# A graph layer with a guessed order of edges: the verdict on dst over the 180 real groups, and mids cleared first

## The chip, the core and the metric

The kernel runs on one core of a Trainium2 chip, in one launch. The metric is the device time of an execution in microseconds (us). Before the change the median of three executions is 5790.02 us (5788.27 to 5802.1). In the text PE is TensorE, PEld its weight load, DVE VectorE, ACT ScalarE, POOL GpSimd and SP SyncE; a small q behind an engine's name means its sequencer, which issues transfers.

## The reference

One graph layer with 12500 nodes of 128 numbers and 412500 edges of 48 numbers; dst is sorted.

```python
h   = relu(layernorm(x))                                    # 12500 x 128
agg = segment_sum(edge_attr_48, dst, num_segments=12500)    # 12500 x 48
u   = graph_globals[0]                                      # all nodes are in graph 0
z   = concatenate([h, agg, u])
out = x + relu(z @ W1 + b1) @ W2 + b2
```

## The kernel before

The kernel holds two programs for the same result. The **guessed program** (lines 129 to 497) runs first and always. It relies on dst being sorted and nearly evenly spread: edges are taken in chunks of 768 (128 partitions by 6), three chunks make a group, and there are 179 full groups and one tail of 84 edges, `NG = 180` in all. A group's edges are expected to fall into a window of 32 nodes for each chunk. For each group DVE compares the places of the edges inside the window with an iota (`onehot`, line 207), PE multiplies edges with that table (`aggregate`, line 219, 36 instructions in the trace, 18 in the program), and DVE adds the window into `aggT`, the sums by node, at an offset that it reads from the row `at_i` (`add`, line 229). Blocks of 512 nodes go through layernorm and the two matrix products in between (lines 231 to 336), and are stored to `out`.

The **general program** (lines 503 to 609) stands under `tc.If(isbad >= 1)`. It clears `aggT` and recomputes everything without a guess: a loop over 537 chunks (line 569) with an inner loop over windows of 64 nodes (line 556), and then a loop over 125 blocks of 100 nodes (line 577). It writes `out` again.

What decides between them is `bad`, a number that `verdict` (line 379) makes from the table `chk`: the largest entry of each of the 128 rows, summed over the rows by PE and clamped to 0..1. Fourteen of the 15 columns of `chk` hold sums of how far edges fall outside their windows (`outside`, line 186, on ACT). The last column is written by `places` (line 356). It takes the row `mids`, dst in the middle of each group, subtracts the expected middle `cen`, clamps the difference to plus or minus `SLACK = 47`, and puts the largest square of what was cut off into `chk` (line 365). The same lines make `at_i`. These rows have `NGP = 187` places, since `cen` is an iota in rows of 11; there are 180 groups, so seven places are padding.

The order on each engine is that of the code (`tc.manual_schedule`); semaphores hold an instruction until the ones that it depends on are done, and each transfer has one of eight semaphore lanes and waits for the transfer before it on its lane. What matters at the start:

- SP's queue loads the middles `md` and the rows `di` of dst, the edges `e` of the first groups and the block `xt` of x.
- ACT's queue loads `mids` in two pieces (lines 392 and 395). ACT then copies the transposed places of the first 30 chunks to `rel` (line 182), issues eight loads of weights (lines 339 to 347, among them `u`, line 346), and makes the first check (line 188).
- POOL makes the constants, clears `mids` (line 409), `chk` and `w1a`, and then clears `aggT` in 16 pieces (line 426), 14 of them ahead of its first other work.
- DVE makes `df`, the places relative to the window (line 173), the table of group 0 (line 207), then `places` with the cast of `mids` at line 358, then the table of group 1.
- PE transposes `df` (line 181), takes group 0 and group 1, then the product of `u` with its weights (line 353), then group 2.

Of the kernel before, what the change touches and what calls it, by code (L numbers as in the profile page):

```python
# [11 lines left out]
OP = mybir.AluOpType  # L12
AX = mybir.AxisListType
# [8 lines left out]
def kernel(  # L22
# [12 lines left out]
    nc = tc.nc  # L35
# [22 lines left out]
    NG = NGF + 1  # L58
# [71 lines left out]
    with fast:  # L130
# [12 lines left out]
        NCK = 2 * len(parts) + 2  # L143
        chk = one.tile([P, NCK + 1], F32)
        offrow = one.tile([1, 126], F32)
        off = one.tile([126, 1], F32)
        mids = one.tile([1, NGP], I32)
        cen = one.tile([1, NGP], F32)
        dev = one.tile([1, NGP], F32)
        devc = one.tile([1, NGP], F32)  # L150
# [4 lines left out]
        def load_dst(i):  # L155
            c0, rows = parts[i]
            di = dp.tile([126, CE], I32, name="di")
            md = dp.tile([126, 1], I32, name="md")
            with nc.allow_non_contiguous_dma(reason="one number a row"):
                nc.sync.dma_start(  # L160
                    md[:rows],
                    dst[c0 * CE:(c0 + rows) * CE].rearrange("(g e) -> g e", e=GE)[:, GE // 2:GE // 2 + 1]
                    .to_broadcast([rows // CG, CG]))
            nc.sync.dma_start(di[:rows], dst[c0 * CE:(c0 + rows) * CE].rearrange("(c e) -> c e", e=CE))
            dsts[i] = di, md
# [190 lines left out]
        def places():  # L356
            mf = one.tile([1, NGP], F32)
            nc.vector.tensor_copy(mf, mids)
            nc.vector.tensor_tensor(dev, mf, cen, OP.subtract)
            nc.vector.tensor_scalar(devc, dev, float(-SLACK), float(SLACK), OP.max, OP.min)  # L360
            nc.vector.tensor_tensor(mf, devc, cen, OP.add)
            nc.vector.tensor_scalar(at_i, mf, 0.0, float(N - 1), OP.max, OP.min)
            nc.vector.tensor_tensor(dev, dev, devc, OP.subtract)
            nc.vector.tensor_tensor(devc, dev, dev, OP.mult)
            nc.vector.tensor_reduce(chk[0:1, NCK:NCK + 1], devc, AX.X, OP.max)

        def tail_dst():
            di = one.tile([P, T], I32)
# [19 lines left out]
        AHEAD = 9  # L388
        with tc.manual_schedule():
            load_dst(0)  # L390
            with nc.allow_non_contiguous_dma(reason="a number a group, once"):
                nc.scalar.dma_start(
                    mids[:, :NGF],
                    dst[:NGF * GE].rearrange("(a g e) -> a g e", a=1, e=GE)[:, :, GE // 2])
                nc.scalar.dma_start(
                    mids[:, NGF:NG], dst[None, NCH * CE + TAIL // 2:NCH * CE + TAIL // 2 + 1])
# [9 lines left out]
            nc.gpsimd.memset(over, float(1 - W))  # L406
            nc.gpsimd.iota(cen, pattern=[[SPAN, NGP // PER], [EACH, PER]], base=HALF, channel_multiplier=0,
                           allow_small_or_imprecise_dtypes=True)
            nc.gpsimd.memset(mids, 0)
            nc.gpsimd.memset(chk, 0.0)  # L410
            nc.gpsimd.memset(w1a, 0.0)
            warm = one.tile([P, 1], F32)
# [23 lines left out]
            for g in range(3, AHEAD):  # L436
                load(g)
            onehot(0)
            places()
            onehot(1)  # L440
            load_weights()
# [196 lines left out]
```

## Time and profile before

| | |
|---|---|
| median of three executions | 5790.02 us |
| the profiled execution | 5793.29 us |
| its span, first to last instruction | 5791.3 us |
| instructions | 139158 |
| busy: PE, PEld, DVE, ACT, POOL | 1728.0, 1342.1, 1069.6, 352.7, 58.6 us |
| moved from and to memory | 175.00 and 12.80 MB |
| granted TensorE clock, mean | 0.532 |

The profile is of one execution. The busy times are shares of a span that has stages with different limits, so they are read stage by stage: from the span's start, the guessed program, then the general program's preparation, its loop over chunks and its loop over blocks, each a window of time. Lines of the kernel name the stage: numbers under 500 are the guessed program, numbers from 512 on the general one.

### The profile page before, as it was taken

How to read it: one execution, taken by the hardware profiler on the slowest of the kernel's cores; microseconds unless marked ns; L12 is line 12 of the kernel's file. 1: busy time of each engine (PE TensorE's matmuls, PEld its weight loads, DVE VectorE, ACT ScalarE, POOL GpSimd, SP SyncE). 2: the span in 40 equal slices, each digit the busy share in tenths (PEclk: the TensorE clock that was granted, in tenths of full speed). 3: DMA queues.
4: the chain of work that ended last, by engine and by line, in shares of the span. 5: the costliest groups of instructions: out<-in, count | busy, mean ns of one | idle time of the engine just before them, and what ended most of it. 6: DMA issues, size and time to landing. Idle time of an engine off the chain costs nothing. (4 is left out here: it accounts for less than half of the span.)

```text
span 5791.3 us, 139158 instructions
## 1 busy us (share of the span) xinstructions
PE 1728.0 (30%) x15319; PEld 1342.1 (23%) x15320; DVE 1069.6 (18%) x3730; ACT 352.7 (6%) x902; POOL 58.6 (1%) x58
## 2 busy tenths in 40 slices
PE   8962222222222222222222222222223333333333
PEld 6741111111111111111111111111122222222222
DVE  6641111111111111111111111111111111111111
ACT  3320000000000000000000000000001111111111
POOL 2010000000000000000000000000000000000000
PEclk9975555555555555555555555555555555555555
DMA  9830000000000000000000000000000000000000
GB/s 287 277 109 20 20 21 20 20 20 20 20 21 20 20 20 20 20 21 21 20 20 20 20 21 21 20 20 20 20 14 8 8 8 8 8 8 8 8 8 8
DMA packets 186921, 188.97 MB, mean 33 GB/s; under 512 B 16241, under 2 KB 179625, under 8 KB 186843
## 3 DMA queue, kind: packets, MB, share of 16 engines
q1 hardware_dynamic: 185541, 187.36, 10.9%
q8 instruction: 58, 0.95, 0.1%
q10 hardware_dynamic: 1302, 0.49, 0.0%
q14 instruction: 20, 0.16, 0.0%
HBM read 175.00 MB, written 12.80 MB: 32 GB/s over the span
## 5 line engine op out<-in xcount | busy, mean ns | idle before, releaser
L564 PE MATMUL ps<-oh,e 128*48 128x64 f32 x6456 | 815.0, 316 | 3043.1 <-DVE oh L560 3043.1
L564 PEld LDWEIGHTS ps<-oh,e 128*48 128x48 f32 x6456 | 699.9, 198 | 3157.9 <-DVE oh L560 3157.9
L555 DVE TENSOR_SCALAR r<-rel 128x6 f32 x537 | 92.5, 172 | 1323.6 <-PEq L569 1322.8
L592 PE MATMUL pt<-ident,xn 100*128 100x100 f32 x125 | 53.5, 428 | 857.1 <-ACT xn L590 857.1
L560 DVE TENSOR_TENSOR oh<-iota,r 128x384 f32<-128x384 f32 x538 | 300.5, 559 | 18.4
L567 DVE TENSOR_TENSOR aggT<-aggT,ps 48x64 f32 x538 | 115.3, 214 | 902.2 <-PE ps L564 902.2
L558 DVE TENSOR_SCALAR r<-r 128x6 f32<-128x6 f32 x538 | 92.6, 172 | 1013.7 <-DMA e<-in_edge_attr_dram 1010.5
L548 ACT COPY relt<-pt 14x1 f32<-14x1 f32 x6 | 0.9, 148 | 3857.7 <-POOLq L551 3856.4
L592 PEld LDWEIGHTS pt<-ident,xn 100*128 100x128 f32 x125 | 22.7, 182 | 899.4 <-ACT xn L590 899.4
L600 PE MATMUL ph<-hT,w1h 128*128 128x100 f32 x500 | 187.2, 478 | 95.8 <-ACT hid L602 54.3
L601 PE MATMUL ph<-ag,w1a 48*128 48x100 f32 x500 | 186.6, 475 | 0.0
L219 PE MATMUL ps<-oh,e 128*48 128x32 f32 x6456 | 176.0, 212 | 16.6 <-DVE oh L207 11.1
L219 PEld LDWEIGHTS ps<-oh,e 128*48 128x48 f32 x6456 | 161.3, 128 | 63.7 <-issue 24.2
L607 DVE TENSOR_TENSOR ot<-po,xt 100x128 f32<-100x128 f32 x125 | 36.5, 292 | 731.0 <-PE po L605 731.0
L600 PEld LDWEIGHTS ph<-hT,w1h 128*128 128x128 f32 x500 | 125.2, 310 | 157.6 <-ACT hid L602 85.2
L605 PE MATMUL po<-w,hid 128*100 128x128 f32 x500 | 156.7, 469 | 0.0
L207 DVE TENSOR_TENSOR oh<-iota,rel 128x576 f32<-128x576 f32 x179 | 151.0, 844 | 2.4 <-ACT rel L182 2.2
L601 PEld LDWEIGHTS ph<-ag,w1a 48*128 48x128 f32 x500 | 124.8, 310 | 44.4 <-issue 44.4
L605 PEld LDWEIGHTS po<-w,hid 128*100 128x100 f32 x500 | 101.8, 264 | 34.5 <-issue 22.2
L602 ACT ACTIVATE hid<-ph,bias 128x100 f32<-128x100 f32 x250 | 86.0, 344 | 378.9 <-PE ph L601 378.9
L596 DVE COPY ag<-aggT 128x100 f32 x125 | 26.6, 213 | 335.1 <-PEq L577 333.6
L586 ACT ACTIVATE sc<-mv,eps 100x1 f32<-100x1 f32 x125 | 36.8, 295 | 801.9 <-DVE mv L585 801.9
(103 smaller groups left out, 892.0 us busy)
## 6 DMA issues: line engine op xcount, KB each, us to landing
e<-in_edge_attr_dram SPq DMA_DIRECT2D x179, 432.0 KB
e<-in_edge_attr_dram SPq DMA_DIRECT2D x537, 144.0 KB
xt<-in_x_dram SPq DMA_DIRECT2D x125, 50.0 KB
out_dram<-ot SPq DMA_DIRECT2D x125, 50.0 KB
xt<-in_x_dram SPq DMA_DIRECT2D x24, 256.0 KB
out_dram<-ot SPq DMA_DIRECT2D x24, 256.0 KB
di<-in_dst_dram SPq DMA_DIRECT2D x4, 384.0 KB
di<-in_dst_dram SPq DMA_DIRECT2D x4, 378.0 KB
```

The lines of the kernel that those rows point to most:

```text
L207: nc.vector.tensor_tensor(oh[:k, :n], iota[:k, None, :W].to_broadcast([k, n, W]), r[:, :, None].to_broadcast([k, n, W]), OP.is_equal)
L219: nc.tensor.matmul(ps[h:h + DE, at:at + W], e[:k, c, t * DE:(t + 1) * DE], oh[:k, c * T + t, :], start=(c == 0 and t < 2), stop=(c == n - ...
L555: nc.vector.tensor_scalar(r[:k], r_view, float(WA), None, OP.add)
L558: nc.vector.tensor_scalar(r[:k], r[:k], float(-WA), None, OP.add)
L560: nc.vector.tensor_tensor(oh[:k], iota[:k, None, :].to_broadcast([k, T, WA]), r[:k, :, None].to_broadcast([k, T, WA]), OP.is_equal)
L564: nc.tensor.matmul(ps, e[:k, t * DE:(t + 1) * DE], oh[:k, t, :], start=(t == 0), stop=(t == T - 1))
L567: nc.vector.tensor_tensor(to, to, ps, OP.add)
L592: nc.tensor.transpose(pt[:, :BA], xn[:BA], ident[:BA, :BA])
L600: nc.tensor.matmul(ph, w1h[:, h * P:(h + 1) * P], hT, start=True, stop=False)
L601: nc.tensor.matmul(ph, w1a[:DE, h * P:(h + 1) * P], ag[:DE], start=False, stop=True)
L602: nc.scalar.activation(hid[:, h], ph, AF.Relu, bias=bias[:, h:h + 1])
L605: nc.tensor.matmul(po[:BA], hid[:, h], w2[:, h], start=(h == 0), stop=(h == NH - 1))
```

## The change

`places` takes the largest square over `devc[:, :NG]`, the 180 real places, and no longer over all 187. The clearing of `mids` stands right behind `load_dst(0)`, ahead of the two loads into `mids` and of all of POOL's other work.

```diff
@@ places()
             nc.vector.tensor_tensor(devc, dev, dev, OP.mult)
-            nc.vector.tensor_reduce(chk[0:1, NCK:NCK + 1], devc, AX.X, OP.max)
+            nc.vector.tensor_reduce(chk[0:1, NCK:NCK + 1], devc[:, :NG], AX.X, OP.max)
@@ the start of the schedule
             load_dst(0)
+            nc.gpsimd.memset(mids, 0)
             with nc.allow_non_contiguous_dma(reason="a number a group, once"):
                 nc.scalar.dma_start(
                     mids[:, :NGF],
...
                            allow_small_or_imprecise_dtypes=True)
-            nc.gpsimd.memset(mids, 0)
             nc.gpsimd.memset(chk, 0.0)
```

On POOL, at the start of the program, before the change (offrow, ones, ident, iota and cen are constants; DMAHW names a transfer's semaphore lane):

```order
L397 ISA
L397 IOTA offrow 1x126
L399 MEMSET ones 128x1
L400 MEMSET ident 128x128
L401 AFFINE_SELECT ident<-ident 128x128 [waits Pool_49]
L403 IOTA iota 128x64
L405 MEMSET eps 128x1
L406 MEMSET over 128x1
L407 IOTA cen 1x187
L409 MEMSET mids 1x187 [waits DMAHW2_49,DMAHW0_49]
L410 MEMSET chk 128x15
L411 MEMSET w1a 128x256
```

And the same place with the change:

```order
L391 MEMSET mids 1x187
L398 ISA
L398 IOTA offrow 1x126
L400 MEMSET ones 128x1
L401 MEMSET ident 128x128
L402 AFFINE_SELECT ident<-ident 128x128 [waits Pool_49]
L404 IOTA iota 128x64
L406 MEMSET eps 128x1
L407 MEMSET over 128x1
L408 IOTA cen 1x187
L410 MEMSET chk 128x15
L411 MEMSET w1a 128x256
```

The clearing of `mids` moved to the front, and with it went POOL's wait for the two loads of `mids`; from `cen` on POOL now waits for nothing. In both programs the first 14 pieces of `aggT` (line 426) are the next rows.

On ACT, the start of its program with the change (w1h to b_sb are weights and biases; pt is the transposed df):

```order
L393 DMA mids<-in_dst_dram 1x179x1 [waits Pool_49]
L396 DMA mids<-in_dst_dram 1x1
L413 ACT_TABLE_LOAD
L413 ACTIVATE warm<-eps 128x1 [waits Pool_49]
L182 COPY rel<-pt 128x3x30 [waits PE_49] x2
L339 DMA w1h<-in_L_gnn_W_dram 128x256 [waits DMAHW4_49]
L340 DMA w1a<-in_L_gnn_W_dram 48x256 [waits DMAHW5_49,Pool_49]
L341 DMA w1a<-in_L_gnn_W_dram 48x256 [waits DMAHW7_49]
L342 DMA w1u<-in_L_gnn_W_dram 64x256 [waits DMAHW0_49]
L343 DMA w_71<-in_L_gnn_W_dram 128x2x128 [waits DMAHW1_49]
L345 DMA b_sb<-in_L_gnn_b_dram 128x2x1 [waits DMAHW3_49]
L346 DMA u<-in_L_gnn_graph_globals_dram 64x1 [waits DMAHW4_49]
```

Its order is as before; what is new is that the first load of `mids` waits for POOL, and that lanes have changed hands (line 341 waited for lane 6 before).

On DVE, around the cast of `mids` (mf is its copy in f32), before with a minus and after with a plus:

```order
-L171 TENSOR_TENSOR sub<-md,off 30x1 [waits DMAHW1_49,DVE_49]
-L173 TENSOR_SCALAR df<-di,sub 30x768 [waits DMAHW3_49,DVE_49]
+L171 TENSOR_TENSOR sub<-md,off 30x1 [waits DMAHW0_49,DVE_49]
+L173 TENSOR_SCALAR df<-di,sub 30x768 [waits DMAHW2_49,DVE_49]
 L207 TENSOR_TENSOR oh<-iota,rel 128x576 [waits Activation_49,Pool_49]
-L358 CAST mf<-mids 1x187 [waits DMAHW2_49,DMAHW0_49,Pool_49]
-L359 TENSOR_TENSOR dev<-mf,cen 1x187 [waits DVE_49]
+L358 CAST mf<-mids 1x187 [waits DMAHW3_49,DMAHW1_49]
+L359 TENSOR_TENSOR dev<-mf,cen 1x187 [waits DVE_49,Pool_49]
```

Nothing moved on DVE: the cast waits for the loads of `mids` alone, where it waited for POOL's clearing too.

## Rows read from the trace of the kernel before

**Rows 1.** The page's first line: span and instructions.

```profile
span 5791.3 us, 139158 instructions
```

**Rows 2.** Windows by stage: us, busy us (instructions) of each engine, PEclk, DMA share, GB/s.

```profile
32.00:365.00 333.00, 321.56 (x6901) 245.40 (x6898) 223.09 (x617) 117.35 (x222) 33.88 (x24) 1.00 0.80 260
...
414.00:4277.00 3863.00, 816.05 (x6462) 700.44 (x6462) 600.94 (x2152) 0.89 (x6) 0.00 (x0) 0.50 0.07 20
4277.00:5788.00 1511.00, 557.76 (x1625) 374.58 (x1625) 199.55 (x875) 214.70 (x625) 0.00 (x0) 0.50 0.03 8
```

**Rows 3.** Page, costliest groups: busy us, mean ns, idle before, who ended it.

```profile
L564 PE MATMUL ps<-oh,e 128*48 128x64 f32 x6456 | 815.0, 316 | 3043.1 <-DVE oh L560 3043.1
...
L555 DVE TENSOR_SCALAR r<-rel 128x6 f32 x537 | 92.5, 172 | 1323.6 <-PEq L569 1322.8
```

**Rows 4.** The instructions of line 503: ns min/median/max, first and last start.

```profile
L503 SPq COMPARE_BRANCH  x1: 49/49/49, 364.6 to 364.6; - x1
```

**Rows 5.** Timeline, first 17 us, ACT's queue and POOL: start us, us, instruction, idle before.

```profile
0.79 1.26 ACTq L392 DMA_DIRECT2D mids<-in_dst_dram  x1
...
2.52 0.71 POOL L407 IOTA cen<- 1x187 f32 x1
...
5.74 0.24 POOL L409 MEMSET mids<- 1x187 int32 x1 [2.51 <-DMA mids<-in_dst_dram]
...
6.23 9.81 POOL L426 MEMSET aggT<- 128x788 f32 x14
```

**Rows 6.** Timeline, first 20 us, DVE.

```profile
4.13 0.61 DVE L173 TENSOR_SCALAR df<-di,sub 30x768 f32<-30x768 int32 x1 [0.63 <-DMA di<-in_dst_dram]
...
6.94 0.76 DVE L207 TENSOR_TENSOR oh<-iota,rel 128x576 f32<-128x576 f32 x1 [2.20 <-ACT rel L182]
7.61 8.54 DVE L358 CAST mf<-mids 1x187 f32<-1x187 int32 x1
...
18.47 1.40 DVE L207 TENSOR_TENSOR oh<-iota,rel 128x576 f32<-128x576 f32 x2
```

**Rows 7.** Timeline, 361 to 390 us, POOL's clearing and two casts of DVE.

```profile
361.24 10.60 POOL L512 MEMSET aggT<- 128x12604 f32 x1 [22.87 <-DVE ot L329]
...
367.82 4.43 DVE L530 CAST df<-di 128x768 f32<-128x768 int32 x1 [4.69 <-DMA e<-in_edge_attr_dram]
...
389.27 0.56 DVE L530 CAST df<-di 128x768 f32<-128x768 int32 x1 [4.38 <-PE pt L536]
```

**Rows 8.** Timeline, 6 to 45 us: weights on ACT's queue, and PE and POOL behind them.

```profile
6.52 0.38 ACTq L339 DMA_DIRECT2D w1h<-in_L_gnn_W_dram  x1
...
16.25 0.49 ACTq L346 DMA_DIRECT2D u<-L_gnn_graph_globals_dram  x1
...
16.79 0.60 ACTq L347 DMA_DIRECT2D b_sb<-in_L_gnn_b_dram  x1
...
19.26 1.66 PE L219 MATMUL ps<-oh,e 128*48 128x32 f32 x36 [9.86 <-DVE oh L207]
...
20.85 1.01 PE L353 MATMUL po<-u,w1u 64*128 64x1 f32 x4
...
22.76 1.71 POOL L271 TENSOR_TENSOR xb<-xt,b_sb 128x512 f32<-128x512 f32 x1 [6.71 <-DMA b_sb<-in_L_gnn_b_dram]
...
44.02 1.00 PE L219 MATMUL ps<-oh,e 128*48 128x32 f32 x36
```

**Rows 9.** Timeline of SP's queue, 360 to 366 us and the last store.

```profile
361.27 2.63 SPq L336 DMA_DIRECT2D out_dram<-ot  x3
364.80 0.36 SPq L528 DMA_DIRECT2D di<-in_dst_dram  x1
...
5787.35 0.31 SPq L609 DMA_DIRECT2D out_dram<-ot  x1
```

**Rows 10.** Timeline of PE at 64 us; then one load in the chain of waits.

```profile
64.31 0.28 PE L219 MATMUL ps<-oh,e 128*48 128x32 f32 x4 [1.69 <-issue]
...
5777.86 1.74 DMA xt<-in_x_dram
```

## The prediction

> **What bounds the kernel now.** I read the page's groups by line first, then windows by stage, then the timeline at the start and around 361 us. The costliest groups belong to lines 555 and 564 [rows 3], so the general program ran: `bad` was 1. The windows say what it took [rows 2]: 32 to 365 us is the guessed program at its own pace, with PE busy 321.56 of 333 us; 414 to 4277 us the loop over chunks, PE busy 816.05 of 3863 us; 4277 to 5788 us the loop over blocks. The bound in those loops is the chain of one pass after the other, where PE waits 3043.1 us for DVE's tables [rows 3]. SP passes the branch of line 503 at 364.6 us [rows 4]: what lies behind it, 5791.3 - 364.6 = 5426.7 us of the span [rows 1], hangs on one number.
>
> **Why the number was 1, and what it becomes.** In the old order POOL cleared `mids` after its loads had landed: the clearing waits 2.51 us for them [rows 5]. So `places` read 187 zeros, and nearly every distance was cut. The new order lets the loads write last. The seven padded places still hold 0 where `cen` is 12602 to 13022; they alone would give a square above 0, and the other edit leaves them out. Either edit without the other keeps `bad` at 1. With both, the reference's inputs decide. I worked them out from its dst: the 180 real middles lie -33 to +8 from `cen`, inside 47; every edge of the full groups has a place of 2 to 30 in its window of 0 to 31, the tail's 14 to 16. So all 15 columns of `chk` are 0, `bad` is 0, and the branch is taken to the end.
>
> **The sum, from the end.** The last of SP's three stores ends its issue at 361.27 + 2.63 = 363.90 us [rows 9]. In the kernel before, the last store's issue ends at 5787.35 + 0.31 = 5787.66, and the span ends at 5791.3: 3.64 us for landing and closing. The same behind 363.90 gives **367.54**. Reading `bad` and the branch cost SP 0.90 us (363.90 to 364.80), which lies beside the landing of that store; without that cover it would be 0.90 more.
>
> *The jump over the general program*: no row shows a branch taken that far. Bounds: 0 (the entry costs nothing visible, rows 4 and 9), and 2.47 us (a pass of the loop of line 569 ends with its closing waits and a jump back: 1322.8 / 536 [rows 3]). The row nearest in kind is PE's stop of 1.69 us inside a run of equal matmuls, with no releaser [rows 10]. Part of such a stop would be covered by the store's landing; I take 1.2: **368.7**. The Trainium skill ("Runtime: NRT & Kernel Launch", Instruction fetch mechanics) says that a taken branch to code outside the fetched pages stalls for a transfer of the target page; it gives no price, and no run here shows a jump this far.
>
> *The clearing moved first.* POOL gains one instruction of 0.24 us at the front; the first load of `mids`, issued at 0.79, now waits for it and comes some 0.3 us later. That costs nothing: the cast that reads `mids` starts at 7.61, and the loads had landed by 5.74 [rows 5, 6]. The constants come 0.2 us later, beside the wait for `di` that ends at 4.13 [rows 6]. SP's queue keeps its order. The reduction over 180 numbers instead of 187 saves nothing that a row could show.
>
> *What POOL does with the 2.51 us.* POOL's wait is gone, so the clearing of `aggT` starts not at 6.23 but at 6.23 - 2.51 = 3.72, and its 14 pieces last until 13.53 [rows 5]. That is the point of the start, since the trace shows DVE held by such clearings: the cast of 187 numbers took 8.54 us and ended at 16.15, right behind POOL's last piece at 16.04, though the pieces are 14 instructions [rows 5, 6]; the cast at 367.82 took 4.43 us and ended 0.41 behind the clearing of line 512, and the same cast takes 0.56 when POOL rests [rows 7]. The TENSOR_TENSOR of line 207 ran beside a clearing in 0.76 us for 576 numbers. Now `df` (line 173) would start at 4.13, 0.41 us after the clearing has begun. It is a TENSOR_SCALAR, which no row shows beside a clearing. But it takes 0.61 us for 768 numbers, close to the cast's 0.56 for as many and above the pace of line 207, so I place it with the casts: held from 4.13 to about 13.53 + 0.46 = 14.0, 9.3 us late.
>
> The Trainium skill ("SBUF — State Buffer", Who interferes with whom) says that GpSimd and a VectorE cast or tensor_scalar in a two-port mode exclude each other for a whole instruction, and a tensor_tensor is not held by a GpSimd instruction that only writes. The trace agrees for the cast (8.54 us) and for line 207 (0.76 us); by that rule `df` is held, without it the start is early, and the two give the first two cases below.
>
> *What hangs on df.* From its end at 4.74 to the end of the first table at 7.70 it was 2.96 us: now 14.0 + 2.96 = 16.96. The cast is free then; from its end at 16.15 to the next table at 18.47 it was 2.32, so the table of group 1 starts near 17.1 + 2.3 = 19.4 instead of 18.47, and PE's group 1 **1.0 us** later than 19.26 [rows 6, 8]. PE's long wait of 9.86 us before group 1 [rows 8] is the cover that hides most of the 9.3. But ACT's copies of `rel`, and behind them on ACT its eight weight loads, slip by 9.3 too: the first from 6.52 to 15.8. PE's product with `u` stood right behind group 1 at 20.85 with no wait; it would be due at 21.9. `u` is issued behind six loads (about 2.4 us of issue) and after `w1h` has landed, which frees its lane. A landing takes 1.74 us with quiet queues [rows 10] and 5.97 us with full ones (16.79 to 22.76 [rows 8]), so `u` lands between 15.8 + 0.4 + 2 x 1.74 = 19.7 and 15.8 + 0.4 + 2 x 5.97 = 28.1. SP's next loads wait for lanes of these weights, so queues are emptier than before; I take 22.5, 0.6 behind its due time. Together **+1.6 us** for the start, with ends of +1.0 and +7.2.
>
> Behind that PE is the bound [rows 2] and edges are loaded nine groups ahead, so a shift goes through to the end. PE's groups take 1.66 us at 19 us and 1.00 at 44 [rows 8]; should that step not move with the work, the shift shrinks to 0.6 of itself, which is inside the ends.
>
> Sum: 368.7 + 1.6 = 370.3 of span, plus what lies around the span in the profiled execution, 5793.29 - 5791.3 = 2.0: **372.3 us**. The median of the runs stands 0.06% under the profiled execution, 0.2 us here.
>
> **The cases.**
> 1. *General program skipped, df held*: 372.3, with ends 367.5 + 1.0 + 2.0 = 370.5 and 367.5 + 7.2 + 2.5 + 2.0 = 379. Chance 0.71.
> 2. *Skipped, df not held*: DVE's cast is free 2.5 us earlier (13.53 instead of 16.04), group 1 comes at 16.8, and the product with `u`, whose loads stay where they were, holds PE to between 0 and 2.5 us gain. 368.7 + 2.0 - 1.3 = 369.4, with ends 367.0 and 372. For it: no TENSOR_SCALAR beside a clearing is in the trace. Against it: its pace. Chance 0.24.
> 3. *The change doesn't do what it says*: `bad` stays 1 through another cell of `chk`, for example a sum on ACT that isn't exactly 0. For it: the trace has no value of `chk`. Against it: the places above. The time is 5790 plus -1.3 to +1.6. Chance 0.04.
> 4. *Slower*: `bad` stays 1, and the held `df` delays the start with the whole chain of weights behind it. Place: PE's product with `u`; price at most 9.3 us, when nothing covers the slip: 5799, +0.16%. It decides only if `bad` stays 1, since otherwise 5.4 ms go at once, and it counts as slower only from 17.4 us (0.3% of 5790, about what a measurement here can tell from no change) on. Chance 0.01.
>
> Faster by over 0.3% is cases 1 and 2, 0.95; within 0.3% case 3, 0.04; slower 0.01. The predicted time is that of case 1. The range takes the ends of cases 1 and 2, with little chance beyond 378: 366 to 378.
>
> **What would show it.** No line from 512 on in the trace, and a span near 370. Line 173's first TENSOR_SCALAR at about 9.9 us instead of 0.61, ending behind the 14 pieces of `aggT`; if it stays at 0.61, case 2 holds. The cast of line 358 short. ACT's first weight load near 15.8 us, and line 353 waiting for `u`. Between SP's branch and its closing waits, the price of the jump. I am wrong if line 512 appears at all.

## The result, and the profile after

The kernel after takes **369.11 us** (median of four executions, 367.71 to 369.66), the kernel before on the same chip 5791.35 us (5788.27 to 5802.1). The ratio is 0.0637, with a 95% interval of 0.0635 to 0.0639. The forecast was 372.3 us with a range of 366 to 378. The profiled execution took 369.66 us, its span is 367.9 us, so 1.76 us lie around it. One execution of e11 below, 374.13 us with its profile, was in a slower state (1.9% above the fastest of the same kernel) and is left out of the comparisons.

The page of the kernel after: its first line, and the chain of waits by engine and by line.

```profile
span 367.9 us, 16685 instructions
...
PE 90%; DVE 4%; issue 3%; ACT 1%; DMA 1%; SPq 0%; DVEq 0%
PE ps L219 44%; PE po L324 14%; PE ph L300 14%; PE ph L307 11%; PE pt L286 4%; DVE df L173 3%; PE pt L181 2%; DVE oh L207 1%; DMA di<-in_dst_dram 1%; ACT rel L182 0%; ACT hid L314 0%; ACT hT L292 0%; SPq L160 0%; PE po L353 0%; DVE aggT L229 0%
```

Where 139158 instructions ran [rows 1], 16685 are left, and none of lines 512 to 609 is among them: the general program was skipped. (Lines 624 and 633, which still run, belong to the launch and to the program's closing.) What is left is the guessed program, with PE on 90% of the chain. One line of the start stands out in the chain: `df`, line 173, with 3%.

The timeline of the kernel after, DVE in the first 20 us (start us, us, instruction, idle before); it answers to [rows 6].

```profile
4.12 9.06 DVE L173 TENSOR_SCALAR df<-di,sub 30x768 f32<-30x768 int32 x1 [0.88 <-DMA di<-in_dst_dram]
15.38 0.76 DVE L207 TENSOR_TENSOR oh<-iota,rel 128x576 f32<-128x576 f32 x1 [2.19 <-ACT rel L182]
16.05 0.24 DVE L358 CAST mf<-mids 1x187 f32<-1x187 int32 x1
...
18.67 1.41 DVE L207 TENSOR_TENSOR oh<-iota,rel 128x576 f32<-128x576 f32 x2
```

The same stretch, POOL; it answers to [rows 5].

```profile
3.66 10.22 POOL L426 MEMSET aggT<- 128x788 f32 x14
```

The hold went from one instruction to another. `df` started at 4.12, 0.46 us behind the first piece of `aggT`, and took 9.06 us instead of 0.61. The cast, which had taken 8.54 us, now takes 0.24, since it comes when POOL has finished.

The timeline of the kernel after, ACT's queue and then PE, 14 to 34 us; they answer to [rows 8].

```profile
14.96 0.37 ACTq L339 DMA_DIRECT2D w1h<-in_L_gnn_W_dram  x1
...
18.05 0.49 ACTq L346 DMA_DIRECT2D u<-L_gnn_graph_globals_dram  x1
```

```profile
16.19 1.66 PE L219 MATMUL ps<-oh,e 128*48 128x32 f32 x36 [1.27 <-DVE oh L207]
19.46 1.65 PE L219 MATMUL ps<-oh,e 128*48 128x32 f32 x36 [1.61 <-DVE oh L207]
21.04 1.01 PE L353 MATMUL po<-u,w1u 64*128 64x1 f32 x4
21.98 1.66 PE L219 MATMUL ps<-oh,e 128*48 128x32 f32 x36
```

Group 1 starts at 19.46 instead of 19.26 and the product with `u` at 21.04 instead of 20.85, behind no wait: of the 9 us that `df` lost, 0.2 are left on PE.

The end, on SP's queue of the kernel after: the last three stores, then the instructions of line 503 (ns min/median/max, first and last start us). They answer to [rows 9] and [rows 4].

```profile
361.12 2.63 SPq L336 DMA_DIRECT2D out_dram<-ot  x3
```

```profile
L503 SPq EVENT_SEMAPHORE  x9: 17/17/17, 364.9 to 366.1; - x9
...
L503 PEldq COMPARE_BRANCH  x1: 456/456/456, 362.4 to 362.4; - x1
...
L503 SPq COMPARE_BRANCH  x1: 50/50/50, 364.4 to 364.4; - x1
```

The last store's issue ends at 361.12 + 2.63 = 363.75, SP branches at 364.4, and its first instruction on the other side comes at 364.9. That side isn't empty: nine semaphore instructions stand there, until 366.1, before the program closes at 367.9.

### The profile page after: what moved, and what is told of

Read it like the earlier page. It is cut to its first block, busy times and chain, and to the rows that moved or that the text cites. A ratio compares the mean times of both kernels' runs of the same rounds, so it can differ in the third digit from the quotient of the medians.

```text
span 367.9 us, 16685 instructions
## 1 busy us (share of the span) xinstructions
PE 337.5 (92%) x7190; PEld 259.9 (71%) x7191; DVE 245.7 (67%) x661; ACT 126.6 (34%) x241; POOL 46.8 (13%) x57
## 4 chain that ended last, share of the span: by engine, by line
PE 90%; DVE 4%; issue 3%; ACT 1%; DMA 1%; SPq 0%; DVEq 0%
PE ps L219 44%; PE po L324 14%; PE ph L300 14%; PE ph L307 11%; PE pt L286 4%; DVE df L173 3%; PE pt L181 2%; DVE oh L207 1%; DMA di<-in_dst_dram 1%; ACT rel L182 0%; ACT hid L314 0%; ACT hT L292 0%; SPq L160 0%; PE po L353 0%; DVE aggT L229 0%
## 5 line engine op out<-in xcount | busy, mean ns | idle before, releaser
L219 PEld LDWEIGHTS ps<-oh,e 128*48 128x48 f32 x6456 | 161.0, 128 | 55.2 <-issue 26.4
L229 DVE TENSOR_TENSOR aggT<-aggT,ps 112x80 f32 x180 | 42.4, 235 | 68.5 <-PE ps L219 54.0
L314 ACT ACTIVATE hid<-ph,bias 128x512 f32<-128x512 f32 (+1 forms) x50 | 33.9, 678 | 110.5 <-PE ph L307 110.5
L271 POOL TENSOR_TENSOR xb<-xt,b_sb 128x512 f32<-128x512 f32 (+1 forms) x25 | 32.2, 1287 | 290.8 <-DVE ot L329 274.0
L324 PE MATMUL po<-w,hid 128*128 128x128 f32 (+1 forms) x392 | 57.0, 287 | 1.0 <-ACT hid L314 0.7
L300 PE MATMUL ph<-hT,w1h 128*128 128x512 f32 (+1 forms) x100 | 55.0, 631 | 0.0
L307 PE MATMUL ph<-aggT,w1a 112*128 112x512 f32 (+1 forms) x100 | 50.2, 582 | 0.0
L324 PEld LDWEIGHTS po<-w,hid 128*128 128x128 f32 (+1 forms) x392 | 47.8, 191 | 3.4 <-ACT hid L314 1.1
L278 ACT ACTIVATE xn<-xt,sh,sc 128x128 f32<-128x128 f32 (+1 forms) x98 | 40.4, 481 | 16.6 <-DVE sh L265 16.6
L300 PEld LDWEIGHTS ph<-hT,w1h 128*128 128x128 f32 x100 | 14.9, 188 | 1.9
```

The source lines that it names most:

```text
L219: nc.tensor.matmul(ps[h:h + DE, at:at + W], e[:k, c, t * DE:(t + 1) * DE], oh[:k, c * T + t, :], start=(c == 0 and t < 2), stop=(c == n - ...
L229: nc.vector.tensor_tensor(to, to, acc[g % 3][:K2, a:a + w], OP.add)
L271: nc.gpsimd.tensor_tensor(xb[:m, :r], xs[j][:m, :r], b2_sb[:m, None, :].to_broadcast([m, r, D]), OP.add)
L278: nc.scalar.activation(xn[:m, q], xs[j][:m, q], AF.Relu, bias=shift[j][:m, q:q + 1], scale=scale[j][:m, q:q + 1])
L300: nc.tensor.matmul(ph[:, :n], w1h[:, h * P:(h + 1) * P], ht[j][:, :n], start=True, stop=False)
L307: nc.tensor.matmul(ph[:, :n], w1a[:K2, h * P:(h + 1) * P], aggT[:K2, BEFORE + a:BEFORE + a + n], start=False, stop=True)
```

## The experiments

Ratios are to the kernel before on the same chip in the same call, in brackets their 95% interval. e1 to e4 ran on one chip, e5 to e8 on a second, e9 to e11 on a third.

**e1: the slice alone.** The kernel before, with only the reduction changed.

```diff
-            nc.vector.tensor_reduce(chk[0:1, NCK:NCK + 1], devc, AX.X, OP.max)
+            nc.vector.tensor_reduce(chk[0:1, NCK:NCK + 1], devc[:, :NG], AX.X, OP.max)
```

> One part alone: the largest square over the 180 real places, with the clearing of mids left where it was, behind its loads. Theory (both edits are needed): places still reads zeros, real middles up to 12500 are cut, bad stays 1, the general program runs: about 5790 us, lines from 512 on in the trace. Rival (the padded places alone set the verdict): the general program is skipped, about 369 us.

Measured: 5794.95 us, one execution.

**e2: the clearing alone.** The kernel after, with the old reduction over 187 places.

```diff
-            nc.vector.tensor_reduce(chk[0:1, NCK:NCK + 1], devc[:, :NG], AX.X, OP.max)
+            nc.vector.tensor_reduce(chk[0:1, NCK:NCK + 1], devc, AX.X, OP.max)
```

> The other part alone: mids cleared first of all, the largest square over all 187 places. Theory: the seven padded places, 0 against 12602 to 13022, keep bad at 1: about 5790 us, and line 173's first instruction is held for 9 us all the same. Rival (the lost middles alone set the verdict): about 369 us.

Measured: 5791.61 us, one execution. The first lines of the pages of e1 and of e2:

```profile
span 5793.0 us, 139158 instructions
```

```profile
span 5789.9 us, 139157 instructions
```

Both ran the general program. So each edit is worth nothing without the other, and the 5.4 ms belong to the number that the two make together. The two also separate the hold. DVE at the start, in e1 (late clearing) and in e2 (early clearing):

```profile
4.16 0.61 DVE L173 TENSOR_SCALAR df<-di,sub 30x768 f32<-30x768 int32 x1 [0.65 <-DMA di<-in_dst_dram]
...
7.64 8.28 DVE L358 CAST mf<-mids 1x187 f32<-1x187 int32 x1
```

```profile
4.31 8.88 DVE L173 TENSOR_SCALAR df<-di,sub 30x768 f32<-30x768 int32 x1 [1.10 <-DMA di<-in_dst_dram]
```

The cast of e2 takes 0.24 us, as in the kernel after. The hold moves with the clearing, not with the reduction.

**e3 and e4: the order alone.** e3 is the kernel before without line 365, so that it skips the general program with POOL's old order; e4 is the kernel after once more.

```diff
-            nc.vector.tensor_reduce(chk[0:1, NCK:NCK + 1], devc, AX.X, OP.max)
```

> The kernel before with the last column of chk never written (line 365 left out; its sums land at wrong nodes, since mids still reads zeros): the general program is skipped with the clearing in its old place. It prices the moved clearing by itself. Theory (the 9 us for which df is held lie beside PE's wait for the table of group 1 and for u): the same as the changed kernel within 0.5 us, 368.6 to 369.6. Rival (the prediction's +1.6 us at the start is real and something later gives it back): 1.6 us faster, 367.5. In the trace PE's product with u at 20.9 and group 8 near 32.4 us.

> The changed kernel once more, as the measure for the run before it on the same chip. Every theory: 367.7 to 369.7 us, as in its four runs.

Measured: e3 367.1 us (366.42 to 368.89, five executions), 0.0634 [0.0632, 0.0636]; e4 368.82 us (368.76 to 369.67, five), 0.0637 [0.0636, 0.0638]. That e3 skips the general program shows, besides, that the last column of `chk` alone had set `bad`.

By the times the old order is 1.7 us quicker. By the trace the start explains little of it: e3's group 1 on PE, and on DVE the cast and the table of group 1, come at

```profile
19.06 1.66 PE L219 MATMUL ps<-oh,e 128*48 128x32 f32 x36 [9.58 <-DVE oh L207]
```

```profile
7.69 8.70 DVE L358 CAST mf<-mids 1x187 f32<-1x187 int32 x1
...
18.27 1.41 DVE L207 TENSOR_TENSOR oh<-iota,rel 128x576 f32<-128x576 f32 x2
```

which is 0.4 us ahead of the kernel after. And those 0.4 us are not the order's. e3 also lacks the reduction of line 365, which stands on DVE between the cast and this table: from the cast's end to the table it is 1.88 us here, 2.38 in the kernel after and 2.32 in the kernel before [rows 6], which has the old order and the reduction. So e3 and e10 do not test the order alone. Since the rest has no row at the start, both were run again (e10 and e11).

**e5: df in another form.** The kernel after, with line 173 as a TENSOR_TENSOR.

```diff
-            nc.vector.tensor_scalar(df[:rows], di[:rows], sub[:rows], None, OP.subtract)
+            nc.vector.tensor_tensor(df[:rows], di[:rows], sub[:rows].to_broadcast([rows, CE]), OP.subtract)
```

> The changed kernel with df made by a TENSOR_TENSOR (sub broadcast) in place of the TENSOR_SCALAR of line 173. Theory (what POOL's clearing holds is the form of the DVE instruction that runs at the cast's pace): df runs at 4.1 us in about 0.9 us, not held; the cast of line 358 is then the one that is held, from about 7.9 to 13 or 14 us; ACT's first weight load is back near 7 us; PE's group 1 at 16.5 to 17.5, the product with u at its landing near 20; time 0 to 1 us less than the changed kernel. Rival (any DVE instruction that writes 30x768 beside the clearing is held): df held to 13 us again and the time the same.

Measured: 366.86 us (365.31 to 369.48, five), 0.0634 [0.0632, 0.0637]. DVE and then PE at the start of e5:

```profile
4.20 0.94 DVE L173 TENSOR_TENSOR df<-di,sub 30x768 f32<-30x768 int32 x1 [1.08 <-DMA di<-in_dst_dram]
7.34 0.76 DVE L207 TENSOR_TENSOR oh<-iota,rel 128x576 f32<-128x576 f32 x1 [2.20 <-ACT rel L182]
8.02 4.84 DVE L358 CAST mf<-mids 1x187 f32<-1x187 int32 x1
...
16.83 0.96 DVE L173 TENSOR_TENSOR df<-di,sub 126x768 f32<-126x768 int32 x1
```

```profile
16.11 1.66 PE L219 MATMUL ps<-oh,e 128*48 128x32 f32 x36 [6.30 <-DVE oh L207]
18.35 0.98 PE L353 MATMUL po<-u,w1u 64*128 64x1 f32 x4 [0.59 <-DMA u<-L_gnn_graph_globals_dram]
```

With POOL's 14 pieces in the same place, `df` takes 0.94 us as a TENSOR_TENSOR and 9.06 as a TENSOR_SCALAR. The later TENSOR_TENSOR of the same line, at 16.83, when POOL rests, takes 0.96 us for as many numbers in each partition: the first one wasn't held at all. The hold belongs to the form of the instruction, and the next one of a form that can be held, the cast, takes it over for 4.84 us. The time is 2.2 us under that of the kernel after, where 0 to 1 was expected; the two ran on different chips, and their intervals overlap.

**e6: the clearing later.** The kernel after, with all pieces of `aggT` from the third on spread over steps 10 to 23.

```diff
-                at_step(i // 2, zero, i)
+                at_step(i // 2 if i < 2 else 8 + i, zero, i)
```

> The changed kernel with pieces 2 to 15 of the clearing of aggT issued from step 10 on, behind POOL's first sum, so that only two pieces stand at the start. Theory: neither df nor the cast is held (0.6 and 0.24 us), the table of group 1 is ready near 10 us, PE's group 1 at 10 to 11 us; but group 2 stays behind the product with u, whose load is issued near 16 us: line 353 at 19.5 to 20.5, so only 0.5 to 1.5 us less at the end, 367.6 to 368.6. Rival (the clearing is what the start waits for): PE is 8 to 9 us earlier and the time near 361.

Measured: **365.72 us** (364.2 to 367.76, five), 0.0631 [0.0629, 0.0632], the lowest median here. DVE and PE at its start:

```profile
4.24 1.27 DVE L173 TENSOR_SCALAR df<-di,sub 30x768 f32<-30x768 int32 x1 [1.02 <-DMA di<-in_dst_dram]
...
8.38 0.24 DVE L358 CAST mf<-mids 1x187 f32<-1x187 int32 x1
```

```profile
11.78 1.66 PE L219 MATMUL ps<-oh,e 128*48 128x32 f32 x36 [1.61 <-DVE oh L207]
19.10 0.98 PE L353 MATMUL po<-u,w1u 64*128 64x1 f32 x4 [5.66 <-DMA u<-L_gnn_graph_globals_dram]
20.02 1.66 PE L219 MATMUL ps<-oh,e 128*48 128x32 f32 x36
```

`df` is held for about 0.7 us by the two pieces that stayed, the cast not at all, and group 1 is 7.7 us early. But PE then stands 5.66 us at line 353 for `u`, and group 2, queued behind it, is only 2 us early. That is the wait the prediction had named; the kernel after hides it behind the held `df`.

**e7: the weights first as well.** e6 with all eight weight loads ahead of ACT's first work.

```diff
             nc.gpsimd.memset(w1a, 0.0)
+            load_weights()
...
             onehot(1)
-            load_weights()
```

> As the run before, with the eight weight loads issued ahead of the copies to rel and of the edges' loads. Theory (behind the clearing the weights bound the start): u is there by about 10 us, line 353 follows group 1 at 12 to 13 us, and the end comes 5 to 8 us earlier, 361 to 364, if the edges keep up. Rival (the edges' transfers bound the first 30 us): PE waits for e instead, less than 2 us gained.

Measured: 370.65 us (368.46 to 372.25, five): slower than e6 by 5 us, so the expected gain was the wrong sign. ACT and PE at its start:

```profile
4.01 0.46 ACTq L339 DMA_DIRECT2D w1h<-in_L_gnn_W_dram  x1
...
14.16 0.35 ACTq L347 DMA_DIRECT2D b_sb<-in_L_gnn_b_dram  x1
14.54 1.28 ACT L414 ACT_TABLE_LOAD   x1 [14.42 <-DMA e<-in_edge_attr_dram]
...
16.04 0.30 ACT L182 COPY rel<-pt 128x90 f32<-128x90 f32 x1
```

```profile
16.39 0.60 PE L181 MATMUL pt<-ident,df 30*128 30x30 f32 x3 [10.15 <-ACT rel L182]
```

ACT issues in order, and each weight load waits for the transfer before it on its lane: 4.01 to 14.51 us for eight loads. The copy of `rel`, which the first tables need, stands behind them, and PE waits 10.15 us for it.

**e8: without the general program.** The kernel after with the load of `bad` and the block under `tc.If` taken out.

```diff
-    isbad = nc.values_load(bad[0:1, 0:1], min_val=0, max_val=1,
-                           skip_runtime_bounds_check_because="clamped to 0..1 on the chip")
-    with tc.If(isbad >= 1):
...
```

> The changed kernel with the general program, the load of bad and the branch left out. It prices the branch and the jump that the changed kernel still pays. Theory (SP's load and branch lie beside the last store's landing, the jump about 0.5 us): 0 to 1 us less, 368 to 369. Rival (the jump's price of 1.2 us and more is hidden in the closing): 1.5 to 2.5 us less, 366.6 to 367.6.

Measured: 366.21 us (365.39 to 366.89, five), 0.0632 [0.0631, 0.0633]. Its span and its last stores:

```profile
span 364.4 us, 16646 instructions
```

```profile
359.76 2.62 SPq L336 DMA_DIRECT2D out_dram<-ot  x3
```

From the end of the last store's issue, 362.38, to the end of the span it is 2.0 us, where the kernel after takes 367.9 - 363.75 = 4.15. In e4, the kernel after once more, it is 367.9 - 364.16 = 3.74. A skipped `tc.If` at the end therefore costs **1.7 to 2.1 us** here. In the kernel after these are, in order, the reading of `bad` and the branch (363.75 to 364.4), the jump (0.5), and the semaphore instructions behind it (364.9 to 366.1); how much of it lies beside the landing of the store isn't shown. The median is 2.9 us under that of the kernel after, more than the theory (0 to 1) and the rival (1.5 to 2.5) had; what lies beyond the closing is not explained, and the two ran on different chips.

**e9: the product with u later as well.** e6 with line 353 at step 5 instead of step 2.

```diff
-            at_step(2, bias_of_globals)
+            at_step(5, bias_of_globals)
```

> The kernel with the late clearing of aggT (e6), and in addition the product of u with its weights (L353) taken at step 5 in place of step 2. Theory (PE's queue): in e6 PE stood 5.66 us at L353 for the load of u, with group 2 queued behind it; with L353 behind groups 2 to 4, group 2 starts at 14 to 16 us in place of 20.02, L353 waits for nothing, and the end moves by as much less what the next wait takes: 360 to 364 us against 365.72. Rival (the loads): the edges of groups 3 to 8 land from 9.5 to 23 us one lane after another, as in e6, so that PE, freed at L353, stops two or three groups later for edges or for the tables that ACT and DVE make; then PE's idle time between 13 and 31 us stays near the 7 us of e6 and the time is 365 to 367 us.

Measured: 366.78 us (365.0 to 369.39, five), 0.0634 [0.0631, 0.0636]: not told apart from e6. PE and ACT at its start:

```profile
11.79 3.10 PE L219 MATMUL ps<-oh,e 128*48 128x32 f32 x72 [1.62 <-DVE oh L207]
...
20.77 0.92 PE L181 MATMUL pt<-ident,df 126*128 126x126 f32 x3 [3.45 <-ACT rel L182]
```

```profile
18.03 0.84 ACT L188 ACTIVATE sc<-df 30x768 f32<-30x768 f32 x1 [10.43 <-DMA b_sb<-in_L_gnn_b_dram]
...
19.93 0.79 ACT L182 COPY rel<-pt 128x378 f32<-128x378 f32 x1
```

The rival holds in the time and in the kind of stop, on ACT, though PE's idle time between 13 and 31 us is halved (3.45 us, 6.63 in e6) where the rival had it unchanged: group 2 comes right behind group 1, but two groups later PE waits 3.45 us for the next `rel`, which on ACT stands behind the last weight load (issued until 17.98) and the check of line 188. Windows of 20 to 66 us, in the kernel after and in e9 (columns as in [rows 2]), show where the rest of the lead goes:

```profile
20.00:66.00 46.00, 43.76 (x938) 35.00 (x936) 31.73 (x90) 16.27 (x33) 8.03 (x7) 1.00 0.99 310
```

```profile
20.00:66.00 46.00, 40.61 (x864) 31.89 (x865) 26.75 (x77) 15.73 (x30) 16.89 (x19) 1.00 1.05 336
```

In both the transfer engines are busy all the time (0.99 and 1.05), and the kernel that comes earlier keeps PE busy for 3.15 us less. The first 0.77 us of its window are the end of the wait for `rel`. Most of the rest are stops of PE in the middle of its work, with no releaser. These are the ones inside a group of line 219, one in the kernel after (which has another of 1.06 us between two products of line 286) and four in e9:

```profile
47.99 0.77 PE L219 MATMUL ps<-oh,e 128*48 128x32 f32 x26 [1.19 <-issue]
```

```profile
42.43 0.77 PE L219 MATMUL ps<-oh,e 128*48 128x32 f32 x26 [0.91 <-issue]
...
49.18 0.55 PE L219 MATMUL ps<-oh,e 128*48 128x32 f32 x16 [1.16 <-issue]
...
55.92 0.41 PE L219 MATMUL ps<-oh,e 128*48 128x32 f32 x10 [0.70 <-issue]
...
62.44 0.28 PE L219 MATMUL ps<-oh,e 128*48 128x32 f32 x4 [1.84 <-issue]
```

A group has 36 of these matmuls, so PE stops with 26, 16, 10 or 4 of a group left, when the group's edges and table are already in use: these are not waits for edges. The four lie 126 matmuls apart, and other runs stop at the same places of the program (with 4 left in the kernel before [rows 10] and in e10). The page of the kernel after has a DMA queue named "instruction" with 58 packets and 0.95 MB, 16 KB each. In the 13 traces, all 46 stops of over 0.55 us inside a group (of the runs with the general program, those ahead of it) end 2.4 to 2.9 us after such a packet began to move. So PE most likely waits there for its own instructions; no run here tests it.

**e10 and e11: the order, a second time.** The kernels of e3 and of the kernel after, beside e9 on a third chip.

> The order of the kernel before without L365 (the largest of the guess's 15 checks is left out, the clearing of mids stays late), a second time, beside the kernel after on one chip. Theory (the start shift is a real cost of the change, as the prediction had it at 1.6 us): again 1 to 2.2 us under the kernel after, near 367.3 us. Rival (the difference of the first call was the spread of single executions): within 0.6 us of the kernel after.

> The kernel after, beside e9 and e10 on one chip. Both theories: 368.5 to 369.7 us. Theory (start shift real): 1 to 2.2 us above e10. Rival: within 0.6 us of e10.

Measured: e10 368.31 us (366.45 to 370.59, five), 0.0636 [0.0634, 0.0638]; e11 369.41 us (367.28 to 371.57, four), 0.0638 [0.0636, 0.0641]. Again the old order is ahead, by 1.1 us, but here the intervals overlap. Two out of two point the same way; but since e3 and e10 lack a reduction too, and the traces show 0.4 to 0.5 us of it at the start, whether the order costs anything stays open. One reason why single executions can't settle it is in e10's own trace, PE at 63 to 70 us and two windows of it:

```profile
63.62 0.28 PE L219 MATMUL ps<-oh,e 128*48 128x32 f32 x4 [1.43 <-issue]
63.84 1.80 PE L300 MATMUL ph<-hT,w1h 128*128 128x512 f32 x2
...
68.31 1.13 PE L300 MATMUL ph<-hT,w1h 128*128 128x512 f32 x2
```

```profile
64.20:67.50 3.30, 3.30 (x10) 0.91 (x10) 1.26 (x5) 0.06 (x1) 0.00 (x0) 0.50 1.06 352
67.60:73.00 5.40, 5.40 (x118) 4.02 (x114) 2.85 (x12) 1.89 (x5) 0.00 (x0) 1.00 0.73 216
```

Behind a stop of 1.43 us the granted clock is 0.50, the 1.2 GHz level, and the two matmuls of line 300 take 1.80 us where they take 1.13 a little later. Not every stop has that behind it: after the 1.84 us of e9 the granted clock stayed at 1.00 (62 to 70 us). At the same place of the program PE stops for 1.69 us in the kernel before [rows 10], for 1.27 us in e4 and for 1.84 us in e9, and not in the kernel after or in e3. Such stops differ from one execution to the next by more than the 0.4 us in dispute at the start.

## Why the prediction was right, and where it was off

**The number that decides.** Right: `bad` is 0 and nothing of the general program ran. e1 and e2 confirm the step that either edit alone keeps it at 1, and e3 that the last column of `chk` alone had set it. Cases 3 and 4 are gone.

**The hold of df.** Right in kind and nearly in size: 4.12 to 13.18 where 4.13 to 14.0 was forecast. The release comes 0.8 us earlier since DVE got in ahead of the 14th piece, not behind it: `df` ends 0.4 us behind the 13th, and POOL's 14 pieces take 10.22 us instead of 9.81, since the last one is now held in its turn. Why DVE gets in there, and not between other pieces, isn't shown. So case 1 is what happened, though the time, 369.1, is nearer to the 369.4 of case 2 and lies below case 1's own lower end, 370.5; the range holds it only because it takes in case 2, and the time alone would have named the wrong case. The Trainium skill ("SBUF — State Buffer", Who interferes with whom) has the pair of rules on which the two cases stood, and the runs agree with both: 9.06 us for the tensor_scalar in the kernel after, 0.94 for the tensor_tensor in e5 beside the same clearings. It speaks of one whole instruction; in the trace DVE waited through 13 of them in a row.

**The sum.** Three terms are off, in the profiled execution, all to the high side:

| term | predicted | measured | difference |
|---|---|---|---|
| end of the last store's issue, start shift included | 363.90 + 1.6 = 365.5 | 363.75 | -1.75 |
| closing and jump | 3.64 + 1.2 = 4.84 | 4.15 | -0.69 |
| around the span | 2.0 | 1.76 | -0.24 |
| time | 372.3 | 369.66 | -2.7 |

- *Start shift, mis-sized in this trace.* Of the 1.0 us for group 1 only 0.2 came: 0.8 went with the earlier release. Of the 0.6 us for `u` nothing came: it was issued at 18.05 instead of 16.25 and had landed by 21.04. Emptier queues did more than I had given them. What was left did not reach the end either, since the last stores are 0.15 us *earlier* than in the kernel before. The times are kinder to the term: e3 against e4, and e10 against e11, differ by 1.7 and 1.1 us. But e3 and e10 lack line 365 too, which makes their 0.4 us at group 1; the kernels before and after, which both have it, differ by 0.2. The mechanism that I gave for 1.6 us shows 0.2, and what the medians differ by comes up behind the start and isn't explained.
- *"A shift goes through to the end".* This step holds only roughly. The table has starts of line 219's groups, found by counting its matmuls, 36 to a group, and the end of the last store's issue, in us:

| run | group 2 | group 25 | last store's issue |
|---|---|---|---|
| kernel after | 21.98 | 65.83 | 363.75 |
| e4, the same kernel | 21.98 | 68.16 | 364.16 |
| e3 | 21.59 | 65.08 | 361.34 |
| e6 | 20.02 | 65.51 | 361.97 |
| e9 | 13.25 | 64.56 | 361.01 |

  e6 loses most of the 7.7 us of its group 1 to `u`, ahead of group 2, and from there its lead over the kernel after is 1.96 us at group 2, 0.32 at group 25 and 1.78 at the end. e9 has 8.73 us at group 2, loses 3.45 of them to ACT's `rel` and about 1 to line 353, which now comes behind group 4, and keeps 1.27 at group 25 and 2.74 at the end. e3's 0.39 becomes 2.41. And e4, which starts as the kernel after does, is 2.33 us late at group 25 and 0.41 at the end. PE's later stops thus take up or add up to 2.3 us, more than the shift that the prediction carried through them; that the sum for the last store, 365.5, came within 1.8 us of 363.75 and 1.3 of 364.16 is in part luck.
- *Jump.* The branch itself costs about 0.5 us, not 1.2. But the estimate left out what e8 shows: the other side of the branch has work of its own, and the whole of a skipped block is 1.7 to 2.1 us. The sum came close by luck, because the old closing of 3.64 us, taken over from before, had such work in it too: behind the last store of the kernel before, SP passes a branch and eight semaphore instructions of the block loop's line 577, from 5787.8 to 5789.4. The Trainium skill ("Runtime: NRT & Kernel Launch", Instruction fetch mechanics) says that a taken branch out of the fetched pages stalls. The trace fits that, with 0.45 us on SP from the branch to its next instruction, and with 456 ns for PE's branch, which took 98 ns in the kernel before; that a fetch is what they wait for isn't shown.

**Terms put at nothing.** This held: the clearing of `mids`, the later first load of `mids`, the constants and the shorter reduction show no cost in any row.

## What to carry to other kernels

Before anything in a guarded kernel is tuned, look in the costliest groups of the profile for lines of the fallback: a guard that always fires hides behind a program that is merely slow. A clearing that is moved forward takes its contention along; ask which instruction of DVE now starts beside it, and in which form. And a gain at the start is worth only what the next wait leaves of it: price the second wait, not only the one that goes.

## What was not expected of the hardware

- A run of 14 clearings on POOL holds one DVE instruction through 13 of them: 9.06 us for a TENSOR_SCALAR of 768 numbers in the kernel after, 8.88 in e2. In the trace the pieces overlap by some 0.05 us (0.745 us long, a new one about every 0.70), and DVE isn't let in between the first 13. That the clearing comes in pieces did not help DVE there; spreading the pieces out (e6) did.
- The block that is branched over costs 1.7 to 2.1 us at the end of this program, of which the jump, 0.5 us, is the smaller part.
- PE stops for 0.6 to 1.8 us in the middle of runs of equal matmuls, at the same places of the program in several runs, 2.4 to 2.9 us after a 16 KB packet of the instruction queue began to move. Which of these places cost time differs from one execution to the next.
